# Last layer of a four-layer network: softmax bias, norms and expert weights on GpSimd, the experts' last product on VectorE

## The chip, the cores and the metric

The kernel runs on one core of a Trainium2 chip. The metric is the time of one execution on the device in microseconds (us); the time given is the median of several executions. Engines are named as the profile names them: PE is TensorE (PEld its weight loads), DVE is VectorE, ACT is ScalarE, POOL is GpSimd, SP issues the transfers. PSUM is the memory that PE writes; in this kernel's last layer it is used as eight banks of 128 x 512 numbers. The granted clock of PE is printed in every profile as a share of full speed.

## What is computed

The network has four layers; each adds a cross-attention block and then a feed-forward block to x, which is 2048 rows (16 tiles of 128) by 256. Only the last layer is touched:

```python
# cross-attention: 16 heads of 16, every row attends to all 2048 rows of ctx
q, k, v = _fq_sym(q * scale, -1), _fq_sym(k, -1), _fq_sym(v, 2)   # quantised to +-127
attn = softmax(q @ k.T)
attn = _fq_unsigned(attn, -1)                                     # quantised to 0..255 by its row's maximum
x = x + (attn @ v) @ Wp + bp
# mixture of experts: 8 experts of width 176, and 2 shared ones
probs = softmax(h @ gate_w.T);  w, selected = top_k(probs, 2)     # h: layernorm of x
w = w / (w.sum(-1) + 1e-20)
y_e = (silu(h @ gate_e.T) * (h @ up_e.T)) @ down_e.T              # every expert on every row
x = x + sum over e of combine[e] * y_e                            # shared experts have weight 1
```

## The kernel before

The last layer is the function `l3`, which begins about 1825 us into the execution and runs to its end. Its order is written out by hand for all engines (`manual_schedule`), so every engine works through its instructions in the order of the Python code.

The main loop `for u in range(N + 29)` runs over N = 256 pairs of a tile t and a head: u = 16 t + head. One pass is called a **round** here, and round h of a tile means u mod 16 = h. A softmax row has 2048 scores, which fill four banks; each quarter is a **piece** q = 0..3. In round u the engines get, in this order:

- ACT: four exponentials of head u (`exponentials`, L976), one for each piece, with the bias `nb` of that head. The result is rounded to 16-bit integers, and a transposing DMA from SP turns it (L980).
- PE: pieces 2 and 3 of head u+1 (`scores`, L954). DVE: their row maxima, negated (`peak`, L960), and then `bias` of head u+1: the smallest of the four columns of `nm` (L965), times the row's scale plus a constant (L966). The exponentials of round u+1 need it.
- the steps of the table `steps` that are due for some tile in this round (below).
- PE: the product of head u-4 with the values (`values`, L988), then pieces 0 and 1 of head u+2. DVE: the maximum of piece 0 of head u+2, then the second half of an expert if there is one (`rest`), then the maximum of piece 1.

Seven banks go round among the pieces and all other products. `take` chooses the free bank whose estimated return (`give`) is earliest. While an expert runs, its bank, given back in `rest` as u + 1.1, is the one that piece 2 of the next round takes.

The steps of tile t, at rounds counted from 16 t: -16 `stats`, -15 `norm` (L1003), -14 `turn_h`, -13 `project_q`, -12 `quant_q` (with four wide POOL operations and a memset, L1034 to L1039), -6 `turn_q`; 20 `divide` (L1055 to L1060), 21 `turn_o`, 22 `project_o`, 23 `stats_m`, 24 `norm_m` (L1089), 25 `turn_m`, 27 `logits`, 28 `top`, 29 `combine` (L1118 to L1125); 30 to 39 the ten experts; 33, 36, 39, 40 `turn_a`, the transposes of the experts' results `act`; 40, 41, 43, 44 `down`, the last projection.

So round h of the loop holds, for three tiles at different stages: h = 14, 15, 0 to 7 one expert each; beside it in h = 0 `stats`, 1 `turn_a` and `norm`, 2 `turn_h`, 3 `project_q`, 4 `turn_a`, `divide` and `quant_q`, 5 `turn_o`, 6 `project_o`, 7 `turn_a` and `stats_m`; h = 8 `turn_a`, `down`, `norm_m`; 9 `down`, `turn_m`; 10 `turn_q`; 11 `down`, `logits`; 12 `down`, `top`; 13 `combine`.

An expert is: PE multiplies into one bank `gu` (gate in the left half, up in the right, L243); ACT writes tanh of the left half to `ma` (L1133) and the right half times the expert's weight to `mb` (L1134); DVE makes (ma + 1) * left half (L1137); POOL multiplies that by `mb` into `act` (L1138). The order of a round's work with an expert in it, as in the code:

```python
for f in steps.get(...): later.append(f(t, u))     # PE: gu; ACT: ma, mb
values(u - LAG)                                    # PE
for q in range(2): scores(u + 2, q)                # PE: pieces 0 and 1
peak(u + 2, 0)                                     # DVE
for f in later: f()                                # DVE: L1137, POOL: L1138 (rest)
peak(u + 2, 1)                                     # DVE
```

The feed-forward block of the first layer (L441 to L443) already computes its experts with ACT for the tanh alone and two DVE products, both of 128 x 176.

Of the kernel before, what the change touches and what calls it, by code (L numbers as in the profile page):

```python
# [18 lines left out]
F32 = mybir.dt.float32  # L19
BF16 = mybir.dt.bfloat16  # L20
# [4 lines left out]
AF = mybir.ActivationFunctionType  # L25
ALU = mybir.AluOpType
AX = mybir.AxisListType
PSUM = bass.MemoryType.PSUM

P = 128  # L30
NT = 16
D = 256
NH = 16
T = NT * P

MAGIC = 12582912.0
LN255 = 5.541263545158426
# [3 lines left out]
class Net:  # L41
# [879 lines left out]
    def l3(self, w3, moe_w):  # L921
# [7 lines left out]
        nc, tc = self.nc, self.tc  # L929
        qw, ow, qb, ob, kst, v, sv = (w3[n] for n in ("q", "o", "qb", "ob", "k", "v", "sv"))  # L930
        gate_w, wgu, wd = moe_w
        NE, IN = 10, 176
        LAG = 4
        E = mybir.EngineType
        with (self.pool("l3x", bufs=2) as pool, self.pool("l3p", bufs=3) as pp,
              self.pool("l3t", bufs=LAG + 1) as tp, self.pool("l3m", bufs=1) as mp,
              self.pool("l3e", bufs=3) as ep):
            st = {}
# [3 lines left out]
            def take(shape, name, dtype=F32):  # L942
                tag = min(banks, key=banks.get)
                del banks[tag]
                return self.bank(shape, tag, name, dtype), tag

            def give(tag, when):
                banks[tag] = when


            def scores(u, q):
                t, hd = divmod(u, NH)
                ps, tag = st["s", u, q] = take([P, 512], "piece")
                nc.tensor.matmul(ps, qTs[t % 2][:, hd, :],  # L954
                                 kst[q // 2][:, hd // 2, 512 * (q % 2):512 * (q % 2) + 512], start=True, stop=True)

            def peak(u, q):
                if q == 0:
                    st["nm", u] = self.s(4, "nm")
                nc.vector.tensor_reduce(st["nm", u][:, q:q + 1], st["s", u, q][0], AX.X, ALU.max, negate=True)  # L960

            def bias(u):
                t, hd = divmod(u, NH)
                nb = st["nb", u] = self.s(1, "nb")
                nc.vector.tensor_reduce(nb, st.pop(("nm", u)), AX.X, ALU.min)  # L965
                nc.vector.tensor_scalar(nb, nb, st["sq", t][:, hd:hd + 1], LN255, ALU.mult, ALU.add)  # L966

            def exponentials(u):
                t, hd = divmod(u, NH)
# [30 lines left out]

            def norm(t, u):
                st["h"] = pool.tile([P, D], F32, name="ln_h", tag="ln_h")
                nc.vector.tensor_scalar(st["h"], self.x[t], st["mv"][:, 0:1], st["r"], ALU.subtract, ALU.mult)  # L1003

            def turn(src, n, name, where, u):

# [18 lines left out]
            def quant_q(t, u):  # L1025
                q = st["q"]
                v = q.rearrange("p (h d) -> p h d", d=16)
                am, s4, r, sq = self.s(NH, "ham"), self.s(NH, "hs4"), self.s(NH, "hr"), self.s(NH, "hs")
                nc.vector.tensor_reduce(am, v, AX.X, ALU.max, apply_absolute_value=True)

                nc.vector.tensor_scalar(s4, am, 1.0 / 127.0, 4e-8, ALU.mult, ALU.max)
                nc.vector.reciprocal(r, s4)
                nc.gpsimd.tensor_scalar(sq, s4, 0.25, None, ALU.mult)
                nc.gpsimd.tensor_tensor(v, v, r.unsqueeze(2).to_broadcast([P, NH, 16]), ALU.mult)  # L1034
                nc.gpsimd.tensor_scalar(q, q, MAGIC, None, ALU.add)
                qi = pool.tile([P, NH, 64], BF16, name="qi", tag="qi")
                nc.gpsimd.memset(qi[:, :, 48:], 0.0)
                for j in range(3):
                    nc.gpsimd.tensor_scalar(qi[:, :, 16 * j:16 * j + 16], v, -MAGIC, None, ALU.add)  # L1039
                st["qi"], st["sq", t] = qi, sq  # L1040

            def turn_q(t, u):
                out = qTs[t % 2].rearrange("p (j two) q -> p j two q", two=2)
# [9 lines left out]
            def divide(t, u):  # L1053
                rz, z = self.s(NH, "rz"), st.pop(("z", t))
                nc.vector.tensor_reduce(rz, z, AX.X, ALU.add)  # L1055
                nc.vector.reciprocal(rz, rz)
                nc.vector.tensor_scalar(rz, rz, 2.0 ** 24, None, ALU.mult)
                st["out"] = pool.tile([P, NH, 16], F32, name="o", tag="o")
                nc.vector.tensor_tensor(st["out"], st.pop(("av", t)), rz.unsqueeze(2).to_broadcast([P, NH, 16]), ALU.mult)  # L1059
                nc.gpsimd.tensor_tensor(self.x[t], self.x[t], ob, ALU.add)  # L1060
# [25 lines left out]

            def norm_m(t, u):
                st["mh"] = mp.tile([P, D], F32, name="mh", tag="mh")
                nc.vector.tensor_scalar(st["mh"], self.x[t], st["mmv"][:, 0:1], st["mr"], ALU.subtract, ALU.mult)  # L1089

            def turn_m(t, u):
                st["mhT"] = turn(st["mh"], 2, "mhT", mp, u)
# [21 lines left out]
            def combine(t, u):  # L1114
                best, fidx = st["best"], st["fidx"]

                den, w = self.s(1, "gden"), self.s(2, "gw")
                nc.vector.tensor_scalar(den, best[:, 0:1], best[:, 1:2], 1e-20, ALU.add, ALU.add)  # L1118
                nc.vector.reciprocal(den, den)
                nc.vector.tensor_scalar(w, best[:, :2], den, 0.5, ALU.mult, ALU.mult)  # L1120
                comb, one = mp.tile([P, NE], F32, name="comb", tag="comb", bufs=2), self.s(8, "gone")
                nc.vector.tensor_scalar(comb[:, :8], self.iota[:, :8], fidx[:, 0:1], w[:, 0:1], ALU.is_equal, ALU.mult)
                nc.vector.tensor_scalar(one, self.iota[:, :8], fidx[:, 1:2], w[:, 1:2], ALU.is_equal, ALU.mult)
                nc.vector.tensor_tensor(comb[:, :8], comb[:, :8], one, ALU.add)
                nc.gpsimd.memset(comb[:, 8:], 0.5)  # L1125
                st["comb"] = comb

            def expert(e):
                def step(t, u):
                    ps, tag = take([P, 2 * IN], "gu")  # L1130
                    self.matmul_acc(ps, [(st["mhT"][:, c, :], wgu[:, c, e, :]) for c in range(2)])
                    a, b = (ep.tile([P, IN], F32, name=n, tag=n) for n in ("ma", "mb"))
                    nc.scalar.activation(a, ps[:, :IN], AF.Tanh, scale=0.5)  # L1133
                    nc.scalar.activation(b, ps[:, IN:], AF.Identity, scale=st["comb"][:, e:e + 1])  # L1134

                    def rest():
                        nc.vector.scalar_tensor_tensor(a, a, 1.0, ps[:, :IN], ALU.add, ALU.mult)  # L1137
                        nc.gpsimd.tensor_tensor(act[:, e * IN:(e + 1) * IN], a, b, ALU.mult)  # L1138
                        give(tag, u + 1.1)
                    return rest  # L1140
                return step
# [7 lines left out]
            def down(k):  # L1149
                def step(t, u):  # L1150
# [7 lines left out]
                    if k == 3:  # L1158
# [3 lines left out]
                return step  # L1162


            steps = {-16: [stats], -15: [norm], -14: [turn_h], -13: [project_q], -12: [quant_q], -6: [turn_q],
                     20: [divide], 21: [turn_o], 22: [project_o],
                     23: [stats_m], 24: [norm_m], 25: [turn_m], 27: [logits], 28: [top], 29: [combine]}
            for e in range(NE):
# [7 lines left out]
            act = mp.tile([P, 14 * P], F32, name="act", tag="act")  # L1176
# [2 lines left out]
            qTs = [mp.tile([P, NH, P], BF16, name=f"qT{j}", tag=f"qT{j}") for j in range(2)]  # L1179
            with tc.manual_schedule(engines={E.PE, E.DVE, E.Activation, E.Pool, E.SP}):  # L1180
                nc.gpsimd.memset(act[:, NE * IN:], 0.0)
                for qT in qTs:
                    nc.gpsimd.memset(qT, 0.0)
                for n in sorted(n for n in steps if n < 0):
                    for f in steps[n]:
                        f(0, -1)
                for q in range(4):
                    scores(0, q)
                    peak(0, q)
                bias(0)  # L1190
                for q in range(2):
                    scores(1, q)
                    peak(1, q)
                for u in range(N + 29):
                    if u < N:
                        exponentials(u)
                    if u + 1 < N:
                        for q in (2, 3):
                            scores(u + 1, q)
                            peak(u + 1, q)  # L1200
                        bias(u + 1)
                    later = []
                    for t in range(NT):
                        for f in steps.get(u - NH * t, ()) if u - NH * t >= 0 or t > 0 else ():
                            later.append(f(t, u))
                    if 0 <= u - LAG < N:
                        values(u - LAG)
                    for q in range(2):
                        if u + 2 < N:
                            scores(u + 2, q)  # L1210
                    if u + 2 < N:
                        peak(u + 2, 0)
                    for f in later:
                        if f:
                            f()
                    if u + 2 < N:
                        peak(u + 2, 1)
# [83 lines left out]
```

## Time and profile before

| | |
|---|---|
| median of three executions | 2978.15 us (2968.15 to 2980.59) |
| profiled execution, its own time | 2982.18 us |
| span in the profile | 2980.4 us |
| mean granted clock of PE over the span | 0.918 |
| stretch 1850 to 2930 us, 1080 us: busy PE / DVE / ACT / POOL | 837.4 / 873.0 / 929.1 / 177.9 us |
| the same stretch: mean granted clock | 0.89 |

The exponentials of round 0 start at 1849.5 us and those of the last round at 2929.9 us. From one round's first exponential to the next round's, the medians of tiles 4 to 14 are, in us:

| round h | 0 | 1 | 2 | 3 | 4 | 5 | 6 | 7 |
|---|---|---|---|---|---|---|---|---|
| us | 3.74 | 4.20 | 4.01 | 3.76 | 4.76 | 6.19 | 3.75 | 4.77 |

| round h | 8 | 9 | 10 | 11 | 12 | 13 | 14 | 15 |
|---|---|---|---|---|---|---|---|---|
| us | 3.29 | 4.84 | 3.99 | 6.27 | 3.30 | 4.18 | 4.99 | 3.74 |

Four exponentials by themselves take 3.02 to 3.04 us a round (the rounds 0 to 13 of the first tile, where there is little else, are mostly of that length). Sixteen rounds take 68.6 to 71.4 us in tiles 2 to 14. Rounds 5, 11 and 15 differ from tile to tile (5.23 to 6.82, 4.62 to 6.88, 3.73 to 5.27 us); the others hardly do.

In a row of the timeline the columns are: start in us, duration in us, engine, line, operation, out<-in, shape, how many were merged into the row, and in brackets how long the engine stood idle before it and what ended that.

### The profile page before, as it was taken

The numbers are of one execution on the slowest core, as the hardware profiler recorded it, in microseconds if no ns is written. First come the engines' busy times: TensorE is split into PE (matmuls) and PEld (weight loads), VectorE is DVE, ScalarE is ACT, GpSimd is POOL, SyncE is SP. The second block draws the span as 40 slices with busy tenths as digits, with TensorE's granted clock in tenths as the row PEclk, the third lists the DMA queues.
The fourth block names the chain that finished last, engine by engine and source line by source line (L and its number), as shares of the span: only waits on it lengthen the run. The fifth ranks groups of instructions, "written<-read, shape, count | busy, mean of one in ns | idle before, by whom it ended". The sixth has DMA issues, their size and how long they took to land. (4 is left out here: it accounts for less than half of the span.)

```text
span 2980.4 us, 41726 instructions
## 1 busy us (share of the span) xinstructions
PE 2462.4 (83%) x14070; PEld 1558.7 (52%) x14070; DVE 1969.7 (66%) x5045; ACT 1758.9 (59%) x4636; POOL 1000.2 (34%) x1587
## 2 busy tenths in 40 slices
PE   5888998999999877888888885777777777777778
PEld 4555666666666544456555652344444444444445
DVE  4555665655665634566666644987887788777774
ACT  1344444444444432555555542988888888888884
POOL 4443444444443322555555531111111111121111
PEclk8889999999999898899999996689999899899999
DMA  6000000000001011000000003876766666666672
GB/s 207 1 1 1 1 1 1 1 1 1 1 1 36 23 35 41 5 5 5 5 5 5 1 1 94 154 130 122 129 125 122 122 123 128 121 125 117 122 128 57
DMA packets 559830, 171.38 MB, mean 58 GB/s; under 512 B 538912, under 2 KB 555904, under 8 KB 558848
## 3 DMA queue, kind: packets, MB, share of 16 engines
q1 hardware_dynamic: 559616, 168.72, 28.0%
q8 instruction: 111, 1.82, 0.2%
q14 instruction: 103, 0.84, 0.1%
HBM read 32.37 MB, written 2.10 MB: 12 GB/s over the span
## 5 line engine op out<-in xcount | busy, mean ns | idle before, releaser
L976 ACT ACTIVATE p<-piece,nb,hs 128x512 int16<-128x512 f32 x1024 | 785.3, 791 | 27.6 <-issue 16.9
L960 DVE TENSOR_REDUCE nm<-piece 128x1 f32<-128x512 f32 x1024 | 651.9, 684 | 110.0 <-PE piece L954 101.6
L954 PE MATMUL piece<-kst,qT 128*128 128x512 bf16 x1024 | 367.9, 415 | 200.9 <-DVE ma L1137 89.3
L1138 POOL TENSOR_TENSOR act<-ma,mb 128x176 f32<-128x176 f32 x160 | 89.1, 558 | 764.1 <-DVE ma L1137 763.1
L243 PE MATMUL gu<-w_L_ffn_wgu,mhT 128*128 128x352 f32 x640 | 254.1, 526 | 11.5 <-ACT p L976 8.0
L954 PEld LDWEIGHTS <-qT 128*128 128x128 bf16 x1024 | 77.1, 98 | 298.9 <-issue 169.8
L235 ACT COPY pT<-tp 128x512 f32<-128x512 f32 (+1 forms) x208 | 116.1, 563 | 185.1 <-PE tp L219 184.2
L976 ACT ACTIVATION_READ_ACCUMULATOR p<-piece,nb,hs 128x1 f32 x1024 | 222.7, 217 | 0.0
L243 PEld LDWEIGHTS gu<-w_L_ffn_wgu,mhT 128*128 128x128 f32 x640 | 124.3, 208 | 132.2 <-ACT p L976 83.9
L988 PEld LDWEIGHTS <-pT 128*128 128x128 f16 x4096 | 143.9, 99 | 81.8 <-issue 66.7
L270 POOL TENSOR_TENSOR kx<-kT,hmask 128x512 f32<-128x512 f32 x128 | 133.1, 1048 | 152.1 <-PE scores L273 102.3
L534 ACT ACTIVATE s<-s,nb,qs 128x128 f32<-128x128 f32 x256 | 123.2, 482 | 97.5 <-DVE nb L532 95.8
L289 PEld LDWEIGHTS av<-v,pT 128*128 128x128 f32 x1024 | 133.6, 198 | 87.5 <-ACT pT L235 73.3
L243 PE MATMUL gu<-w_L_ffn_wgu,hT 128*128 128x352 f32 x512 | 174.5, 463 | 0.9 <-ACT actT L235 0.6
L289 PE MATMUL av<-v,pT 128*128 128x17 f32 x1024 | 134.8, 263 | 47.8 <-ACT pT L235 47.7
L275 DVE TENSOR_REDUCE mx<-scores 128x4 f32<-128x512 f32 x128 | 88.2, 689 | 120.1 <-PE scores L273 119.6
L280 ACT ACTIVATE p<-scores,mx,qs 128x128 f32<-128x128 f32 x256 | 96.9, 459 | 118.8 <-DVE mx L278 111.2
L988 PE MATMUL av<-v_int,pT 128*128 128x16 bf16 x4096 | 143.4, 171 | 19.3 <-DVE o L1059 19.3
L273 PE MATMUL scores<-kx,qT 128*128 128x512 f32 x256 | 153.8, 686 | 3.1 <-ACT qT L235 2.7
L537 POOL TENSOR_TENSOR s<-s,rz 128x512 f32<-128x512 f32 x64 | 66.7, 1043 | 227.5 <-DVE rz L536 225.2
L549 PE MATMUL oproj<-w_L_ffn_oT,oT 128*128 128x256 f32 x512 | 130.4, 399 | 4.9 <-ACT oT L543 4.8
L243 PE MATMUL q<-w_L_ffn_qT,hT 128*128 128x512 f32 x256 | 126.7, 598 | 2.2 <-DVE rot L488 2.1
(362 smaller groups left out, 5375.4 us busy)
## 6 DMA issues: line engine op xcount, KB each, us to landing
pT<-p SPq DMA_TRANSPOSE x256, 4.3
w_L_ffn_wgu<-in_L_ffn_wgu SPq DMA_DIRECT2D x1, 3520.0 KB, 12.0
w_L_ffn_wgu<-in_L_ffn_wgu SPq DMA_DIRECT2D x1, 2816.0 KB, 9.4
x<-in_x SPq DMA_DIRECT2D x16, 128.0 KB, 4.6
ctxT<-in_ctxT SPq DMA_DIRECT2D x4, 512.0 KB, 5.3
w_L_ffn_qT<-in_L_ffn_qT SPq DMA_DIRECT2D x1, 2048.0 KB, 12.2
w_L_ffn_oT<-in_L_ffn_oT SPq DMA_DIRECT2D x1, 2048.0 KB, 17.1
ctx<-in_ctx SPq DMA_DIRECT2D x16, 128.0 KB, 2.0
```

The source lines that it names most:

```text
L235: nc.scalar.copy(out[:, j0:j0 + m, :], ps)
L243: self.nc.tensor.matmul(ps, a, b, start=(j == 0), stop=(j == n - 1))
L270: nc.gpsimd.tensor_tensor(kx, kT[oc].unsqueeze(1).to_broadcast([P, 4, P]), self.hmask[:, hs].unsqueeze(2).to_broadcast([P, 4, P]), ALU.mult)
L273: nc.tensor.matmul(ps, qT[:, oc, :], kx, start=True, stop=True)
L280: nc.scalar.activation(p[:, h, :], ps[:, h, :], AF.Exp, bias=mx[:, h:h + 1], scale=scale)
L289: nc.tensor.matmul(av[:, 4 * g + h, :], pT[:, h, :], v[:, 4 * g + h, :], start=True, stop=True)
L534: nc.scalar.activation(s[:, j, :], s[:, j, :], AF.Exp, bias=nb[:, j:j + 1], scale=qs[:, j:j + 1], accum_out=z[:, j:j + 1])
L549: nc.tensor.matmul(proj, oT[:, j, :], w["o"][:, c, :], start=(c == 0), stop=(c == 15))
L954: nc.tensor.matmul(ps, qTs[t % 2][:, hd, :], kst[q // 2][:, hd // 2, 512 * (q % 2):512 * (q % 2) + 512], start=True, stop=True)
L960: nc.vector.tensor_reduce(st["nm", u][:, q:q + 1], st["s", u, q][0], AX.X, ALU.max, negate=True)
L976: nc.scalar.activation(p[:, 512 * q:512 * q + 512], ps, AF.Exp, bias=nb, scale=st["sq", t][:, hd:hd + 1], accum_out=st["z", t][:, hd, q:q ...
L988: nc.tensor.matmul(st["av", t][:, hd, :], pb[:, c, :], v[:, c, hd * 16:(hd + 1) * 16], start=(c == 0), stop=(c == NT - 1))
```

## The change

- The running minimum of the four `nm` columns and the bias move to POOL: after the maximum of piece 1 and of piece 2 POOL takes a minimum of two columns into a fifth and sixth column; `bias` becomes two POOL operations (minimum with the last column and product with the scale; plus the constant) in place of two DVE operations.
- `norm` and `norm_m` (layernorm of 128 x 256) move from DVE to POOL.
- In `combine` the four operations after the reciprocal move from DVE to POOL.
- An expert loses ACT's `mb` and POOL's product. DVE makes the second product itself, up half of the bank times the expert's weight times `ma`, straight into `act`.
- `quant_q` is cut in pieces: its last five POOL operations move to the four rounds that follow (`round_q`, `copy_q`).
- The factor 2^24 that `divide` multiplied in once a tile (L1057) goes once into `sv`, before the loop.

```diff
             def peak(u, q):
                 if q == 0:
-                    st["nm", u] = self.s(4, "nm")
-                nc.vector.tensor_reduce(st["nm", u][:, q:q + 1], st["s", u, q][0], AX.X, ALU.max, negate=True)
+                    st["nm", u] = self.s(6, "nm")
+                nm = st["nm", u]
+                nc.vector.tensor_reduce(nm[:, q:q + 1], st["s", u, q][0], AX.X, ALU.max, negate=True)
+                if q in (1, 2):
+
+                    nc.gpsimd.tensor_scalar(nm[:, 3 + q:4 + q], nm[:, q:q + 1], nm[:, 0:1] if q == 1 else nm[:, 4:5],
+                                            None, ALU.min)
 
             def bias(u):
                 t, hd = divmod(u, NH)
                 nb = st["nb", u] = self.s(1, "nb")
-                nc.vector.tensor_reduce(nb, st.pop(("nm", u)), AX.X, ALU.min)
-                nc.vector.tensor_scalar(nb, nb, st["sq", t][:, hd:hd + 1], LN255, ALU.mult, ALU.add)
+                nm = st.pop(("nm", u))
+                nc.gpsimd.tensor_scalar(nb, nm[:, 3:4], nm[:, 5:6], st["sq", t][:, hd:hd + 1], ALU.min, ALU.mult)
+                nc.gpsimd.tensor_scalar(nb, nb, LN255, None, ALU.add)
...
             def norm(t, u):
                 st["h"] = pool.tile([P, D], F32, name="ln_h", tag="ln_h")
-                nc.vector.tensor_scalar(st["h"], self.x[t], st["mv"][:, 0:1], st["r"], ALU.subtract, ALU.mult)
+                nc.gpsimd.tensor_scalar(st["h"], self.x[t], st["mv"][:, 0:1], st["r"], ALU.subtract, ALU.mult)
...
                 nc.gpsimd.tensor_scalar(sq, s4, 0.25, None, ALU.mult)
                 nc.gpsimd.tensor_tensor(v, v, r.unsqueeze(2).to_broadcast([P, NH, 16]), ALU.mult)
+                st["sq", t] = sq
+
+            def round_q(t, u):
+                q = st["q"]
                 nc.gpsimd.tensor_scalar(q, q, MAGIC, None, ALU.add)
-                qi = pool.tile([P, NH, 64], BF16, name="qi", tag="qi")
+                qi = st["qi"] = pool.tile([P, NH, 64], BF16, name="qi", tag="qi")
                 nc.gpsimd.memset(qi[:, :, 48:], 0.0)
-                for j in range(3):
-                    nc.gpsimd.tensor_scalar(qi[:, :, 16 * j:16 * j + 16], v, -MAGIC, None, ALU.add)
-                st["qi"], st["sq", t] = qi, sq
+
+            def copy_q(j):
+                def step(t, u):
+                    v = st["q"].rearrange("p (h d) -> p h d", d=16)
+                    nc.gpsimd.tensor_scalar(st["qi"][:, :, 16 * j:16 * j + 16], v, -MAGIC, None, ALU.add)
+                return step
...
                 nc.vector.reciprocal(rz, rz)
-                nc.vector.tensor_scalar(rz, rz, 2.0 ** 24, None, ALU.mult)
...
-                nc.vector.tensor_scalar(st["mh"], self.x[t], st["mmv"][:, 0:1], st["mr"], ALU.subtract, ALU.mult)
+                nc.gpsimd.tensor_scalar(st["mh"], self.x[t], st["mmv"][:, 0:1], st["mr"], ALU.subtract, ALU.mult)
...
-                nc.vector.tensor_scalar(w, best[:, :2], den, 0.5, ALU.mult, ALU.mult)
+                nc.gpsimd.tensor_scalar(w, best[:, :2], den, 0.5, ALU.mult, ALU.mult)
...
-                nc.vector.tensor_scalar(comb[:, :8], self.iota[:, :8], fidx[:, 0:1], w[:, 0:1], ALU.is_equal, ALU.mult)
-                nc.vector.tensor_scalar(one, self.iota[:, :8], fidx[:, 1:2], w[:, 1:2], ALU.is_equal, ALU.mult)
-                nc.vector.tensor_tensor(comb[:, :8], comb[:, :8], one, ALU.add)
+                nc.gpsimd.tensor_scalar(comb[:, :8], self.iota[:, :8], fidx[:, 0:1], w[:, 0:1], ALU.is_equal, ALU.mult)
+                nc.gpsimd.tensor_scalar(one, self.iota[:, :8], fidx[:, 1:2], w[:, 1:2], ALU.is_equal, ALU.mult)
+                nc.gpsimd.tensor_tensor(comb[:, :8], comb[:, :8], one, ALU.add)
...
-                    a, b = (ep.tile([P, IN], F32, name=n, tag=n) for n in ("ma", "mb"))
+                    a, w = ep.tile([P, IN], F32, name="ma", tag="ma"), st["comb"][:, e:e + 1]
                     nc.scalar.activation(a, ps[:, :IN], AF.Tanh, scale=0.5)
-                    nc.scalar.activation(b, ps[:, IN:], AF.Identity, scale=st["comb"][:, e:e + 1])
 
                     def rest():
                         nc.vector.scalar_tensor_tensor(a, a, 1.0, ps[:, :IN], ALU.add, ALU.mult)
-                        nc.gpsimd.tensor_tensor(act[:, e * IN:(e + 1) * IN], a, b, ALU.mult)
+                        nc.vector.scalar_tensor_tensor(act[:, e * IN:(e + 1) * IN], ps[:, IN:], w, a, ALU.mult, ALU.mult)
                         give(tag, u + 1.1)
...
-            steps = {-16: [stats], -15: [norm], -14: [turn_h], -13: [project_q], -12: [quant_q], -6: [turn_q],
+            steps = {-16: [stats], -15: [norm], -14: [turn_h], -13: [project_q], -12: [quant_q], -11: [round_q],
+                     -10: [copy_q(0)], -9: [copy_q(1)], -8: [copy_q(2)], -6: [turn_q],
...
                 nc.gpsimd.memset(act[:, NE * IN:], 0.0)
+                nc.vector.tensor_scalar(sv, sv, 2.0 ** 24, None, ALU.mult)
```

The order of instructions on PE, and so the bank that each product takes, is the same in both kernels.

## The prediction

> **What bounds the kernel.** The last layer, 1849 to 2930 us, is nearly all that the change touches. Busy shares (ACT 929, DVE 873, PE 837 of 1080 us) name no bound; the medians of the rounds do: with one expert and little else a round takes 3.74 us, though four exponentials need 3.03. I read the timeline of all engines for such a round (15), then the list of waits.
>
> ```profile
> 2306.48 0.59 PE L954 MATMUL piece<-kst,qT 128*128 128x512 bf16 x2
> ...
> 2306.90 0.69 DVE L960 TENSOR_REDUCE nm<-piece 128x1 f32<-128x512 f32 x1 [0.43 <-PE piece L954]
> 2307.50 0.33 DVE L1137 SCALAR_TENSOR_TENSOR ma<-ma,gu 128x176 f32<-128x176 f32 x1
> ...
> 2307.89 0.61 PE L954 MATMUL piece<-kst,qT 128*128 128x512 bf16 x2 [0.81 <-DVE ma L1137]
> ...
> 2308.53 1.45 PE L243 MATMUL gu<-w_L_ffn_wgu,mhT 128*128 128x352 f32 x4
> ...
> 2310.07 0.32 ACT L1133 ACTIVATE ma<-gu 128x176 f32<-128x176 f32 x1
> ...
> 2310.22 0.59 PE L954 MATMUL piece<-kst,qT 128*128 128x512 bf16 x2
> 2310.29 0.40 ACT L1134 ACTIVATE mb<-gu,comb 128x176 f32<-128x176 f32 x1
> ...
> 2310.58 0.78 ACT L976 ACTIVATE p<-piece,nb,hs 128x512 int16<-128x512 f32 x1
> ```
> ```profile
> PE piece L954 <- DVE ma L1137: 88.0, 137, 0.9
> PE piece L954 <- ACT p L976: 73.7, 158, 1.5
> ```
>
> Two loops close at 3.74 us. **The bank loop**: piece 0 (2306.48), its maximum (+0.42), the expert's DVE product (+0.60), which frees the bank that piece 2 of the next round takes (+0.39), those two pieces (to the next expert's gu, +0.64), gu and the values, then piece 0 again (+1.69). **The ACT loop**: second exponential, its bank to gu, gu, `ma`, `mb`, exponential. PE stands idle 0.81 us each time for L1137, and gu follows the pieces within 0.03 (2308.50, 2308.53): the bank loop has at most 0.03 us to spare. What the reader is to see: DVE and ACT both have idle time in this round, and yet the round is as long as the chain through the one bank.
>
> **The second product, the main term.** The bank is now free only after two DVE products. The trace holds the same pair, on the same shape, in the first layer's feed-forward:
>
> ```profile
> 417.25 0.34 DVE L442 SCALAR_TENSOR_TENSOR ma<-ma,gu 128x176 f32<-128x176 f32 x1 [0.46 <-ACT ma L441]
> 417.63 0.40 DVE L443 SCALAR_TENSOR_TENSOR act<-ma,comb,gu 128x176 f32<-128x176 f32 x1
> ```
>
> The second starts 0.38 after the first and takes 0.40: the release comes 0.78 after L1137's start and not 0.33, **0.45 later**. Bounds: 0.25 (the spacing of DVE operations that don't depend on each other, L1137 to the next maximum) to 0.55 (0.10 for the two waits of the new product, on the first product and on POOL's `comb`). I take the pair's own spacing, since it is the same two operations. Behind the piece that waits stand, on PE, piece 3, the next gu, the values and the next piece 0, so the whole round moves with it; behind the new product DVE has only the maximum of piece 1, which is not late. Round by round, from piece 0 to piece 0, 0.45 less the slack of gu after the pieces (it waited for ACT there, which gets earlier):
> - to rounds 15, 0, 1: slack 0.03, so 3 x 0.42.
> - to 2 and 3: slack 0.11 (pieces done 2316.38, gu 2316.49), so 2 x 0.34.
> - to 4: the values wait for `o` of `divide` (PE idle 1.18). DVE's chain gains 0.45, loses the two bias operations (0.32, 2257.47 to 2257.79) and L1057 (0.21): -0.08. PE's own work before the values ends at 2257.92, 0.45 later still before `o`.
> - to 5 and 7: no slack, 2 x 0.45. To 6: slack 0.32, 0.13.
> - to 8: the transposes no longer wait for POOL's product, and the bank of `down` waits for an exponential anyway: 0.
>
> Sum 2.89 us a tile. ACT's loss of `mb` (0.29 from its start to the next, 2310.29 to 2310.58) lies beside this: the ACT loop shrinks to 3.45 and ACT waits the rest of the new 4.16. POOL's product (0.56) goes too; POOL is busy 178 of 1080 us, and nothing in the loop but round 8's transposes waited for it.
>
> **The bias on POOL.** Before, from the end of the last maximum to the exponential: 0.04 + 0.20 + 0.21 + 0.09 = 0.54. On POOL: 0.09 to start (ln_mv to L187), two dependent operations of 0.26 and 0.20 with 0.08 between (L187 takes 0.19; a 128x1 product, L747, 0.24), 0.09 to ACT: 0.72, bounds 0.60 and 1.2 (POOL's cost of a several-fold wait isn't shown). In expert rounds ACT waits for gu far longer. The exponentials wait for the bias at the ends of rounds 9 and 12, +0.18 each, and of 13, where DVE's chain loses 0.33 of the earlier bias: -0.15. Sum +0.21. The running minima wait for DVE's maxima, with the bias queued behind them; 0.09 + 0.26 after each maximum, they are done before the last one ends, 0.63 after its predecessor.
>
> **The rest costs nothing.** The layernorms take 0.94 on POOL (below) for 0.40 on DVE; their transposes come 3.4 us later or more. Without that cover, 0.5 each. `combine` takes some 1.2 us on POOL for 1.3 on DVE, and the first second product comes 4 us later. `quant_q`'s tail, 0.86 + 0.31 + 3 x 0.85, ends in round 8 instead of 5, `turn_q` in round 10; in one piece it would have held up the bias behind it by 3.7 us. POOL has per round four small operations (0.9) and at most 1.8 of these: under 4.16, and each batch starts just after a bias. No DMA is moved.
>
> ```profile
> L735 POOL TENSOR_SCALAR k<-k,n 128x256 f32<-128x256 f32 x16 | 15.1, 941 | 0.2
> ```
>
> Here the Trainium skill speaks against the change: GPSIMD Engine Reference, section 4.1, sends elementwise work to VectorE, GpSimd being about 2 times slower with two inputs and at line rate with one. With one tensor input this row is 2.3 times L1003 (404 ns). By the rule the norm costs 0, by the row 0.54; hidden both ways.
>
> **Ends.** The prologue's norm is bare: +0.5. After the last exponential three waits of PE for `act` (2964.94, 2969.58, 2970.76) lose `mb` and POOL's 0.56 and gain one DVE product, about -0.6 each; `combine` there is +0.4. Together -0.9.
>
> **Sum.** 14 tiles have their experts inside the loop (tile 14 has two in it, where no pieces follow, and tile 15 none): 14 x (2.89 + 0.21) = 43.4; less 0.9, +42.5. The profiled execution's own 2982.2 becomes 3024.7; it lies 4.0 above the median shown, so the median becomes **3021 us**.
>
> **The clock.** PE's idle gap grows from 0.81 to 1.26. Windows of 3.413 us, cut at the multiples at which the granted clock switches:
>
> ```profile
> 2306.44:2309.85 3.41, 2.56 (x18) 1.06 (x15) 2.91 (x7) 3.41 (x10) 0.56 (x1) 1.00 0.76 146
> 2350.81:2354.22 3.41, 1.98 (x27) 1.13 (x27) 2.50 (x6) 3.41 (x10) 0.00 (x0) 1.00 0.47 90
> 2354.22:2357.64 3.42, 2.61 (x7) 1.69 (x7) 3.29 (x6) 3.08 (x9) 0.00 (x0) 0.50 0.82 158
> 2214.28:2217.69 3.41, 2.00 (x29) 1.29 (x28) 2.41 (x6) 3.41 (x8) 0.00 (x0) 1.00 0.55 87
> 2217.69:2221.11 3.42, 3.16 (x31) 2.39 (x30) 2.51 (x7) 2.20 (x9) 0.00 (x0) 1.00 0.65 135
> ```
>
> After window and length come PE's busy us; near the end PEclk. 1.98 busy is followed by half clock, 2.00 is not; in this layer the edge lies near 0.60 of a window. TensorE: Matmul & The Clock Gate (HAM oscillation) warns of idle gaps over some 3.4 us: by it a gap of 1.26 costs nothing. By the trace an expert window falls from 2.56 to (3.41 - 1.29) = 2.12, 0.62: just above the edge, so I take 0, but 0.08 us more gap would cross it.
>
> **Rivals.**
> - *Clock cascade.* For: that margin. Against: by the matmuls' rows, four of five windows between 0.61 and 0.63 in this layer were followed by full clock. A round at half clock takes 5.26 (2232.48 to 2237.74), so 5.7 with the product, 1.5 above 4.16. With four more such rounds a tile, 14 x 4 x 1.5 = 84: 3105.
> - *ACT sets the pace, faster.* For: ACT is the busiest, and the chain of waits is mostly exponentials. If the bank of the expert weren't the one PE waits for, 0.29 would go in each of 140 expert rounds: 2978 - 41 = 2937. It decides if the added DVE time in the loop is under 0.03 us. Against: 137 waits for L1137, 88 us.
> - *Bias late.* If the POOL chain takes 1.2, rounds 9, 12 and 13 lose 0.5 more: 14 x 1.5 = 21, so 3042. For: four dependent operations in one queue. Against: POOL is nearly idle.
> - *The change doesn't do what it says*: no sign of it; PE's order is unchanged, and ACT, DVE and POOL hold the operations that the diff names.
>
> **Chances.** Forecast 0.56, cascade 0.19, bias late 0.09, ACT pace 0.11, the terms cancelling within 0.5% (15 us, what a measurement of this kernel can tell from none) 0.05. Slower 0.84, same 0.05, faster 0.11. The forecast's own range is 2996 (0.25 for the product: 1.16 a tile in place of 2.89) to 3040 (0.55: 3.89 a tile, 3035, and the clock a little worse). That holds the bias case nearly too. Reaching half into the cascade above, and a little into the cancelling case below, the range is 2992 to 3090; outside lie the ACT pace and the long half of the cascade.
>
> **What would show it.** PE's idle before the pieces of an expert round, behind the new product, should be about 1.26, the expert round 4.16, ACT idle 0.7 before `ma` there, round 13 a little shorter, PEclk near 0.89. Wrong if expert rounds shrink to 3.45; if pieces wait less than 1.0; if half-clock windows crowd the rounds 14 to 2; if exponentials wait for POOL in expert rounds.

## The result, and the profile after

The changed kernel takes **3008.6 us** (median of 6 runs, 3003.48 to 3014.78), the kernel before 2975.8 us beside it (6 runs, 2968.15 to 2981.78): ratio 1.0121, 95% interval 1.0100 to 1.0142. It is 33 us slower; the forecast was 43. The profiled execution has a span of 3013.1 us for 2980.4, so the two traces differ by 32.7 us. Of that, 35.2 us is there when the last head's piece 0 starts (2958.1 us for 2922.9); the tail gives 2.5 back.

The timeline of all engines for the same plain expert round that the forecast read (round 15, at full clock; start, duration, engine, line, operation, and in brackets the idle time before it and what ended it):

```profile
2466.94 0.59 PE L954 MATMUL piece<-kst,qT 128*128 128x512 bf16 x2
...
2467.35 0.69 DVE L961 TENSOR_REDUCE nm<-piece 128x1 f32<-128x512 f32 x1 [2.10 <-PE piece L954]
...
2467.96 0.33 DVE L1148 SCALAR_TENSOR_TENSOR ma<-ma,gu 128x176 f32<-128x176 f32 x1
2468.32 0.40 DVE L1149 SCALAR_TENSOR_TENSOR act<-gu,comb,ma 128x176 f32<-128x176 f32 x1
...
2468.64 1.88 DVE L961 TENSOR_REDUCE nm<-piece 128x1 f32<-128x512 f32 x3
...
2468.78 0.60 PE L954 MATMUL piece<-kst,qT 128*128 128x512 bf16 x2 [1.25 <-DVE act L1149]
...
2469.22 1.35 PE L243 MATMUL gu<-w_L_ffn_wgu,mhT 128*128 128x352 f32 x4
...
2470.40 0.55 PE L994 MATMUL av<-v_int,pT 128*128 128x16 bf16 x16
...
2470.60 0.32 ACT L1145 ACTIVATE ma<-gu 128x176 f32<-128x176 f32 x1 [0.52 <-PE gu L243]
2470.72 0.36 POOL L971 TENSOR_SCALAR nb<-nm,hs 128x1 f32<-128x1 f32 x1 [0.36 <-DVE nm L961]
...
2470.81 0.59 PE L954 MATMUL piece<-kst,qT 128*128 128x512 bf16 x2
...
2471.17 0.22 POOL L972 TENSOR_SCALAR nb<-nb 128x1 f32<-128x1 f32 x1
...
2471.42 0.78 ACT L982 ACTIVATE p<-piece,nb,hs 128x512 int16<-128x512 f32 x1 [0.50 <-POOL nb L972]
```

The reader is to see two things. The pieces wait 1.25 us for the second product where they waited 0.81 for the first, and from piece 0 (2466.94) to piece 0 (2470.81) the round takes 3.87 us for 3.74. And a wait is new: the last maximum ends at 2470.52, the bias at 2471.39, and ACT's exponential stands 0.50 us for it.

The list of waits in the stretch from 2000 to 2900 us, first PE's, then ACT's (us in total, times, longest):

```profile
PE piece L954 <- DVE act L1149: 146.1, 121, 1.4
PE piece L954 <- ACT p L982: 64.0, 128, 1.4
```
```profile
ACT ma L1145 <- PE gu L243: 92.3, 104, 2.6
ACT p L982 <- POOL nb L972: 53.0, 92, 0.9
```

In the same stretch of the kernel before, the same two waits were shorter, and no exponential waited for a bias:

```profile
PE piece L954 <- DVE ma L1137: 82.8, 129, 0.9
```
```profile
ACT ma L1133 <- PE gu L243: 60.0, 57, 2.6
```

The windows view of the last layer shows PE, DVE and ACT less busy than before, POOL more, and the same mean clock, 0.89:

```profile
1850.00:2960.00 1110.00, 812.47 (x6553) 471.84 (x6553) 814.30 (x1638) 895.90 (x2331) 449.49 (x1293) 0.89 0.66 122
```

**How rounds are compared below.** From each trace I took the time from piece 0 of one round to piece 0 of the next, and how much of it lay in windows at half clock. Medians over those instances of a round (tiles 2 to 14) that have no half clock in them agree between kernels to 0.02 us where nothing was changed (rounds 10 and 11: 5.08 us, and 3.39 to 3.41, in every kernel with spare matmuls below). So they show what an edit does by itself; the half-clock time, given in us a tile (mean of tiles 3 to 13), stands beside them. "From 14 to 15" means from piece 0 of round 14 to piece 0 of round 15.

### The profile page after: what moved, and what is told of

Read it like the earlier page. It is cut to its first block, busy times and chain, and to the rows that moved or that the text cites. A ratio compares the mean times of both kernels' runs of the same rounds, so it can differ in the third digit from the quotient of the medians.

```text
span 3013.1 us, 42599 instructions
## 1 busy us (share of the span) xinstructions
PE 2440.6 (81%) x14070; PEld 1561.2 (52%) x14070; DVE 1919.9 (64%) x4582; ACT 1723.5 (57%) x4476; POOL 1266.9 (42%) x2547
## 3 DMA queue, kind: packets, MB, share of 16 engines
q8 instruction: 111, 1.82, 0.2%
## 4 chain that ended last, share of the span: by engine, by line
PE 54%; DVE 22%; ACT 11%; POOL 7%; issue 4%; DMA 1%; DVEq 0%; SPq 0%; ACTq 0%; POOLq 0%
PE gu L243 10%; DVE nm L961 8%; PE tp L219 6%; ACT p L982 5%; PE piece L954 4%; PE oproj L549 4%; PE q L243 4%; PE scores L273 4%; PE av L289 3%; PE moe L1168 3%; PE moe L243 2%; PE out L243 2%; PE oT L541 2%; DVE act L1149 2%; PE av L994 2%
## 5 line engine op out<-in xcount | busy, mean ns | idle before, releaser
L964 POOL TENSOR_SCALAR nm<-nm 128x1 f32<-128x1 f32 x512 | 145.0, 283 | 533.3 <-DVE nm L961 530.0
L982 ACT ACTIVATION_READ_ACCUMULATOR p<-piece,nb,hs 128x1 f32 x1024 | 208.2, 203 | 0.0
L243 PEld LDWEIGHTS gu<-w_L_ffn_wgu,mhT 128*128 128x128 f32 x640 | 133.5, 215 | 102.7 <-ACT p L982 44.3
L971 POOL TENSOR_SCALAR nb<-nm,hs 128x1 f32<-128x1 f32 x256 | 93.2, 364 | 93.6 <-DVE nm L961 58.4
## 6 DMA issues: line engine op xcount, KB each, us to landing
w_L_ffn_qT<-in_L_ffn_qT SPq DMA_DIRECT2D x1, 2048.0 KB, 11.5
```

Source lines behind the costliest of these rows:

```text
L243: self.nc.tensor.matmul(ps, a, b, start=(j == 0), stop=(j == n - 1))
L964: nc.gpsimd.tensor_scalar(nm[:, 3 + q:4 + q], nm[:, q:q + 1], nm[:, 0:1] if q == 1 else nm[:, 4:5], None, ALU.min)
L982: nc.scalar.activation(p[:, 512 * q:512 * q + 512], ps, AF.Exp, bias=nb, scale=st["sq", t][:, hd:hd + 1], accum_out=st["z", t][:, hd, q:q ...
```

## The experiments

All times are medians; before was run beside each group (2975.96 for e1 to e4, 2976.28 for the first four kernels with spare matmuls, 2972.64 for nomb and the two with the bias on VectorE, 2973.32 for w_early). Before itself differs by up to 3.6 us between these groups, so a difference of kernels from two groups is good to some 4 us.

| kernel | time us | ratio to before, 95% interval | half clock, us a tile | full-clock rounds, us a tile |
|---|---|---|---|---|
| before | 2975.8 | | 11.5 | |
| the change | 3008.6 | 1.0100 to 1.0142 | 10.6 | |
| e1_product | 2991.3 | 1.0041 to 1.0078 | 7.8 | |
| e2_no_product | 2966.2 | 0.9954 to 0.9982 | 7.5 | |
| e3_bias | 3039.0 | 1.0199 to 1.0237 | 16.1 | |
| e4_early | 3005.7 | 1.0077 to 1.0111 | 15.5 | |
| w_before | 2947.8 | 0.9892 to 0.9919 | 2.2 | 66.35 (65.88) |
| w_after | 2959.4 | 0.9937 to 0.9962 | 0.0 | 68.18 |
| w_e1 | 2968.7 | 0.9962 to 0.9987 | 2.2 | 67.98 (67.64) |
| w_e2 | 2928.6 | 0.9825 to 0.9854 | 0.0 | 65.75 |
| nomb | 2935.4 | 0.9842 to 0.9904 | 7.1 | |
| w_after_dvebias | 2954.6 | 0.9935 to 0.9966 | 1.6 | 67.51 |
| w_rest_dvebias | 2924.7 | 0.9815 to 0.9865 | 1.2 | 65.58 |
| w_early | 2973.0 | 0.9994 to 1.0021 | 5.1 | 66.20 |

The last column is left empty where some round of a tile never ran, or hardly ever, at full clock. In w_before and w_e1 the spare matmuls themselves lengthen the round from 14 to 15 (4.21 us for 3.74 and 3.87 at full clock without them); in brackets stands the sum with that taken out.

### The parts of the change, one at a time

**e1_product**: the kernel before, with the expert of the changed kernel.

```diff
-                    nc.scalar.activation(b, ps[:, IN:], AF.Identity, scale=st["comb"][:, e:e + 1])
...
-                        nc.gpsimd.tensor_tensor(act[:, e * IN:(e + 1) * IN], a, b, ALU.mult)
+                        nc.vector.scalar_tensor_tensor(act[:, e * IN:(e + 1) * IN], ps[:, IN:], w, a, ALU.mult, ALU.mult)
```

> The kernel before with the second product alone moved to VectorE (mb and POOL's product gone, bias, norms and combination as before). Bank theory (the later release of the expert's bank is the cost): the 2.89 us a tile of the forecast, and 0.5 more to round 4, because the divide keeps the bias operations ahead of it: 14 x 3.4 less 1.8 at the end, +46, about 3022. PE's wait for the new product about 1.25 us each time. If the bias on POOL were the larger cost of the change, this kernel would lie under 2990.

Measured 2991.3: 15 above before, a third of what I expected. The pieces wait as long as foreseen (148.8 us in 127 waits), but the rounds grow less, and half clock fell from 11.5 to 7.8 us a tile.

**e2_no_product**: the changed kernel with the expert as before (the diff above, the other way round).

> The changed kernel with the expert's product as before (mb on ACT, last product on POOL), all else of the change kept. Bank theory: within 6 us of before (2970 to 2982), since only 0.21 us a tile is left for the bias and the divide gets earlier by about 0.5. If the bias on POOL is what costs, it stays near 3000. Exponentials waiting for POOL's bias: at the ends of rounds 9 and 12 only.

Measured 2966.2: 10 faster than before, just under the range. ACT did wait for the bias in more places than I named (29.5 us in 58 waits). Here too half clock fell, to 7.5 us a tile. The two parts add up to +5, the whole change is +33: something that doesn't add is at work.

**e3_bias**: the kernel before with `peak` and `bias` of the changed kernel, nothing else.

> The kernel before with minimum and bias alone on POOL. Bank theory: +0.18 at two rounds of a tile, -0.3 at the divide: 2970 to 2980. Bias theory: four dependent POOL operations make every exponential that follows ma late, 0.4 us in some ten rounds of a tile, +50, about 3025.

Measured 3039.0, worse than either theory allowed, and for neither's reason. The timeline of POOL at round 4 to 5, with the exponential that follows:

```profile
2500.28 0.87 POOL L1041 TENSOR_SCALAR q<-q 128x256 f32<-128x256 f32 x1
2501.09 0.31 POOL L1043 MEMSET qi<- 128x256 bf16 x1
2501.37 2.49 POOL L1045 TENSOR_SCALAR qi<-q 128x256 bf16<-128x256 f32 x3
2503.83 0.56 POOL L1144 TENSOR_TENSOR act<-ma,mb 128x176 f32<-128x176 f32 x1
2504.37 0.68 POOL L964 TENSOR_SCALAR nm<-nm 128x1 f32<-128x1 f32 x2
2505.16 0.37 POOL L971 TENSOR_SCALAR nb<-nm,hs 128x1 f32<-128x1 f32 x1
2505.61 0.23 POOL L972 TENSOR_SCALAR nb<-nb 128x1 f32<-128x1 f32 x1
...
2505.87 0.78 ACT L982 ACTIVATE p<-piece,nb,hs 128x512 int16<-128x512 f32 x1 [1.20 <-POOL nb L972]
```

The tail of `quant_q` holds POOL's queue for 3.55 us (2500.28 to 2503.83), and the minima and the bias stand behind it. PE runs short meanwhile, half clock rises to 16.1 us a tile, and the round from 5 to 6 takes 8.07 us (mean) for 4.78. With the tail cut into four rounds (e2) the same bias leaves the kernel 10 faster than before. e2 differs from e3 in the norms, `combine` and the scale of `divide` too, so the cut by itself was not tried; but the timeline shows nothing else of that length ahead of the bias.

### The bank freed early

**e4_early**: the changed kernel, with the product taken in another order.

```diff
-                    a, w = ep.tile([P, IN], F32, name="ma", tag="ma"), st["comb"][:, e:e + 1]
+                    a, b = (ep.tile([P, IN], F32, name=n, tag=n) for n in ("ma", "mb"))
                     nc.scalar.activation(a, ps[:, :IN], AF.Tanh, scale=0.5)
+                    nc.vector.tensor_scalar(b, ps[:, IN:], st["comb"][:, e:e + 1], None, ALU.mult)
+                    nc.vector.tensor_tensor(b, ps[:, :IN], b, ALU.mult)
+                    give(tag, u + 1.1)
...
-                        nc.vector.scalar_tensor_tensor(a, a, 1.0, ps[:, :IN], ALU.add, ALU.mult)
-                        nc.vector.scalar_tensor_tensor(act[:, e * IN:(e + 1) * IN], ps[:, IN:], w, a, ALU.mult, ALU.mult)
-                        give(tag, u + 1.1)
+                        nc.vector.scalar_tensor_tensor(act[:, e * IN:(e + 1) * IN], a, 1.0, b, ALU.add, ALU.mult)
```

> The changed kernel with the expert's product taken in another order: VectorE multiplies the up half by the weight and then by the gate half as soon as gu is there, which frees the bank without waiting for the maximum of piece 0; (tanh + 1) times that comes where the second product was. VectorE does three operations for an expert where the change does two, about 0.33 us more. Bank theory: PE no longer waits for the product, an expert round falls to 3.5 to 3.75 us (ACT's 4 exponentials and ma, 3.4, with the handshakes; or VectorE's 2.5 + 1.1), so 10 x 14 x 0.4 to 0.7 below the changed kernel: 2915 to 2955, below the kernel before too. If VectorE's load as such is the cost, 10 x 14 x 0.33 = 46 above it: about 3055.

Measured 3005.7, level with the change (their ranges overlap): a miss. The waits of PE (2000 to 2900 us) show that the bank did come free early; those of ACT show what took its place:

```profile
PE piece L954 <- DVE mb L1147: 17.0, 55, 0.4
```
```profile
ACT p L982 <- POOL nb L972: 69.2, 104, 1.1
```

Expert rounds now alternate (3.36 us from 14 to 15, in the one instance at full clock, and 4.51 from 15 to 0), and half clock is 15.5 us a tile. Which of the two ate the gain is taken up again below, with w_early.

### The clock taken out

The windows of 3.413 us around round 10 of the kernel before (PE busy, PEld, DVE, ACT, POOL; then the granted clock):

```profile
2490.74:2494.15 3.41, 1.82 (x28) 1.13 (x27) 2.40 (x6) 3.41 (x8) 0.00 (x0) 1.00 0.35 70
2494.16:2497.57 3.41, 3.34 (x10) 2.29 (x7) 2.50 (x6) 1.94 (x6) 0.00 (x0) 0.50 0.81 119
```

PE is busy 1.82 of 3.41 us while ACT runs without a pause; the next window has half clock, and the projection in it pays for it (round 10 takes 6.61 us in the mean, 5.09 at full clock). The next four kernels fill such holes with matmuls that nothing needs:

```diff
+            WARM = {(10, 2): 1, (10, 3): 1, (10, 0): 5, (13, 0): 2, (13, 1): 2, (14, 2): 6, (14, 3): 1}
+            def keep(u, q):
...
+                spare = st["av", t][:, hd + 1:, :].rearrange("p h d -> p (h d)")
+                for _ in range(n):
+                    nc.tensor.matmul(spare, self.ident, wd[:, 0, :m], start=True, stop=True)
...
                             scores(u + 1, q)
+                            keep(u, q)
...
                             scores(u + 2, q)
+                            keep(u, q)
```

> The kernel before with spare matmuls on PE where it waits for ACT in rounds 10, 13 and 14 (18 a tile, fp32, constant operands, into columns of the accumulator of values that a later head writes anew); nothing else is touched and no engine but PE has more to do. Clock theory: windows of 3.413 us in which PE is under some 0.6 busy are followed by half clock, and rounds 10, 13 and 14 pay about 1.5 + 1.3 + 0.5 us a tile for it; with the spare matmuls half-clock time in these rounds falls from 9.0 us a tile to under 3, and the time by 25 to 50: 2925 to 2950. Rival (half clock there costs nothing, because ACT is waited for anyway): 2976 or more.

Measured 2947.8, 28 faster than before. The same round 10, by windows and on PE's timeline:

```profile
2475.99:2479.41 3.42, 3.21 (x31) 2.53 (x28) 2.57 (x5) 3.42 (x9) 0.00 (x0) 1.00 0.71 97
2479.41:2482.82 3.41, 2.99 (x29) 2.00 (x28) 2.50 (x7) 2.19 (x7) 0.00 (x0) 1.00 0.77 156
```
```profile
2476.40 1.39 PE L992 MATMUL av<-w_L_ffn_wd,ident 128*128 128x144 f32 x10
```

The spare matmuls stand in the hole, no half clock follows, and round 10 takes 5.08 us, as it did at full clock without them. The clock theory holds.

> The changed kernel with the same spare matmuls. Clock theory: with the clock out of it the change costs the sum of its full-clock rounds, 2.48 us a tile, 14 x 2.48 = 35 more than the kernel before with spare matmuls (30 to 42). Rival (the clock has no part in the comparison): the same, 33; the pair e1 and e2 tells them apart.

> The second product alone, with the same spare matmuls. Clock theory: its full-clock rounds are 1.71 us a tile longer than before's, so 24 above before with spare matmuls (18 to 30), where without them it was 15. Rival (the product really costs 15, and the other 28 of the change come from the two parts together): 15 again, 12 to 17.

> The change without the product, with the same spare matmuls. Clock theory: its full-clock rounds sum to 0.1 us a tile less than before's, so its lead of 10 over before came from the clock and shrinks to 0 to 4. Rival: 10 faster than before with spare matmuls, as without them.

Measured 2959.4, 2968.7 and 2928.6: 12 above w_before, 21 above it, and 19 below it. Only the product came as expected. The differences of the medians mislead here, because w_before and w_e1 keep 2.2 us a tile of half clock in round 4, where no spare matmul stands, and pay 0.47 and 0.34 us in round 14 for the spare ones, while w_after and w_e2 have neither. The full-clock rounds don't have these flaws: 65.88 before, 67.64 with the product alone (+1.76), 65.75 without it (-0.13), 68.18 for the whole change (**+2.30**). The +1.76 and the -0.13 are the 1.71 and -0.1 that were read before these runs; but at 1.63 together the parts still fall short of 2.30.

### The bias, with and without the product

**w_after_dvebias** and **w_rest_dvebias**: the changed kernel, and the changed kernel without the product, both with spare matmuls, both with `peak` and `bias` as before:

```diff
-                nc.gpsimd.tensor_scalar(nb, nm[:, 3:4], nm[:, 5:6], st["sq", t][:, hd:hd + 1], ALU.min, ALU.mult)
-                nc.gpsimd.tensor_scalar(nb, nb, LN255, None, ALU.add)
+                nc.vector.tensor_reduce(nb, st.pop(("nm", u)), AX.X, ALU.min)
+                nc.vector.tensor_scalar(nb, nb, st["sq", t][:, hd:hd + 1], LN255, ALU.mult, ALU.add)
```

> The changed kernel with spare matmuls, but minimum and bias on VectorE as in the kernel before; product, norms, combination and the split tail of quant_q stay as changed. Theory that the bias on POOL is late by about 0.37 us where an exponential waits for it: rounds 8 and 12 get 0.4 shorter each, 14 and 15 about 0.1, round 3 (divide behind the bias operations) 0.3 longer: 6 below the changed kernel with spare matmuls, 2950 to 2957. Theory that the bias on POOL pays for itself: 2960 or more.

> As the changed kernel without the product and with spare matmuls, but minimum and bias on VectorE too: what is left of the change is norms, combination and quant_q's tail on POOL in pieces, and the scale moved out of divide. If these give what the part without the product gained (19 below before with spare matmuls), about 2930; if it was the bias leaving VectorE ahead of the divide, only round 3's 0.2 is left, about 2944.

Measured 2954.6 and 2924.7. In full-clock rounds the account now closes:

- norms, combination, the cut tail of `quant_q` and the scale out of `divide`: 65.88 to 65.58, **-0.30** us a tile;
- the product on top of that: 65.58 to 67.51, **+1.93**;
- the bias on POOL on top of both: 67.51 to 68.18, **+0.67**; without the product it costs 65.75 - 65.58 = 0.17.

Together +2.30. The bias costs more beside the product. That fits ACT being ready sooner without `mb`: the exponentials waited for it 92 times, with `mb` (e2) 58 times. w_rest_dvebias is the fastest version tried, 1.6% under the kernel before, with w_e2 close to it; half of that or more is the clock (w_before alone gave 0.9%). Of its 23 us under w_before only some 4 are the norms and the rest (0.30 x 14); 0.47 us a tile is w_before's round 14, and 1.0 us a tile less is spent at half clock.

### The bank loop by itself

**nomb**: the kernel before without `mb`.

```diff
-                    nc.scalar.activation(b, ps[:, IN:], AF.Identity, scale=st["comb"][:, e:e + 1])
...
-                        nc.gpsimd.tensor_tensor(act[:, e * IN:(e + 1) * IN], a, b, ALU.mult)
+                        nc.gpsimd.tensor_tensor(act[:, e * IN:(e + 1) * IN], a, a, ALU.mult)
```

> The kernel before without mb: ACT doesn't read the up half, and POOL multiplies ma by itself, so the up half of every expert is left out of the result. What is left at a plain expert round is the bank loop by itself. Theory that gu had 0.20 us of slack behind the pieces (it waited there for ACT's second exponential, 0.64 after piece 2, where 0.44 is enough): 3.74 falls to about 3.54 at full clock, and rounds 14 to 0 with it. The forecast's reading (at most 0.03 of slack): 3.71.

Measured 2935.4, and the rounds from 14 to 0 take 3.44 + 3.61 = 7.05 us at full clock, 3.53 each, for 3.74. PE's timeline of such a round:

```profile
2494.75 0.60 PE L954 MATMUL piece<-kst,qT 128*128 128x512 bf16 x2 [0.81 <-DVE ma L1136]
2495.19 1.35 PE L243 MATMUL gu<-w_L_ffn_wgu,mhT 128*128 128x352 f32 x4
```

`gu` starts 0.44 us after piece 2, before the recorded end of the pieces (2495.35), where it stood at 0.64 in the kernel before. The bank loop had 0.20 us of slack that my reading hid.

The traces of both kernels show the same without nomb, in the row of the weight load of `gu` (PEld), which the forecast's reading left out. First the kernel before in the round that the forecast read, then the changed kernel in the round shown after the result:

```profile
2308.53 0.89 PEld L243 LDWEIGHTS gu<-w_L_ffn_wgu,mhT 128*128 128x128 f32 x4 [0.53 <-ACT p L976]
```
```profile
2469.01 1.00 PEld L243 LDWEIGHTS gu<-w_L_ffn_wgu,mhT 128*128 128x128 f32 x4
```

Before, the weights of `gu` waited for an exponential; after, they follow the pieces without a wait, and `gu` starts 0.44 us after piece 2 (2468.78 to 2469.22). At full clock in tiles 2 to 14 of the kernel before, the medians of that distance are 0.64 us in rounds 0 and 1, 0.69 and 0.70 in rounds 2 and 3 and 0.94 in round 6, always with this wait, and 0.43 to 0.44 without it in rounds 4, 5 and 7. In the changed kernel they are 0.43 to 0.44 in all of these rounds.

### The early bank with the clock taken out

**w_early**: e4_early with the spare matmuls.

> The changed kernel with the product in the other order (bank free early, as in e4) and with the spare matmuls. e4 took the wait for the product away (17 us of PE's waits in place of 146) and was no faster; its full-clock rounds sum to 65.7 us a tile, 2.4 below the changed kernel's 68.2, but it spent 15.5 us a tile at half clock. Theory that half clock ate the gain: with the spare matmuls it is some 30 below the changed kernel with them, 2920 to 2940 (round 4's half clock stays). Theory that the bias on POOL took the product's place as the bound (exponentials waited 69 us for it): 2950 or more.

Measured 2973.0, 14 above w_after (17 by the ratios to before): a miss. The number lies where the second theory put it, but the rounds do not bear that theory out: at full clock, waits for the bias included, they are 2.0 us a tile shorter than w_after's (66.20 for 68.18). But w_early has 5.1 us of half clock a tile left, in rounds where no spare matmul stands (4, 5, 7 and 1; round 7 takes 5.3 us, and 7.2 where a half-clock window falls into it), and w_after has none. Its mean tile is 68.77 us for 68.26. Exponentials wait 75.0 us for the bias (2000 to 2900 us). So half clock took the gain of the full-clock rounds here too; what the waits for the bias cost besides wasn't tried.

## Why the forecast came out as it did

Terms of the forecast beside the full-clock rounds, w_after less w_before, with the flaw of w_before's round 14 taken out (us a tile; the table's round is the one the time leads to):

| to round | 15, 0, 1 | 2, 3 | 4 | 5, 7 | 6 | 8, 9, 10 | 13 | 14 | sum |
|---|---|---|---|---|---|---|---|---|---|
| forecast | 3 x 0.42 | 2 x 0.34 | -0.08 | 2 x 0.45 | 0.13 | 0.18 | 0.18 | -0.15 | 3.10 |
| measured | 0.27, 0.25, 0.21 | 2 x 0.13 | -0.14 | 0.51, 0.44 | -0.08 | 0.37 | 0.38 | -0.16 | 2.31 |

- **The mechanism was right, and shown.** The pieces wait for the second product; the bank comes 0.82 us after the first product's start (2467.96 to 2468.78) where it came after 0.39, 0.43 later for the 0.45 forecast. PE's gap of 1.26 was measured as 1.25.
- **The step that failed** is the slack, "the bank loop has at most 0.03 us to spare". It was read from the recorded end of the pieces; but `gu` waited there for ACT's second exponential, and without `mb` ACT frees that bank earlier. By nomb and by the weight loads the slack is 0.20 us more. The six terms that lean on it (to 15, 0, 1, 2, 3 and 6) make 2.07 us in the forecast and 0.87 with 0.20 taken from each. The product alone (w_rest_dvebias to w_after_dvebias) measures 0.72 for them: 0.20, 0.19 and 0.37 to rounds 15, 0 and 1, 0.06 each to 2 and 3, -0.16 to 6. To rounds 4, 5 and 7, which had no such slack, it measures 0.43, 0.43 and 0.44 for the 0.45 forecast. An expert round at full clock takes 3.87 to 4.0 us, not 4.16.
- **The bias** was put at 0.72 us from the last maximum to the exponential; in the round shown it takes 0.90 (2470.52 to 2471.42: 0.20 to start, 0.36 and 0.22 for the two operations and 0.09 between, 0.03 to ACT). It was also placed wrongly: at the end of round 9, where 0.18 was forecast, it costs nothing (3.36 us to round 10 in w_after and in w_after_dvebias); it costs 0.47 at the end of round 8, which the forecast didn't name, and 0.38 for the 0.18 forecast at the end of round 12. The sign that was to refute the forecast, exponentials that wait for POOL in expert rounds, is there: 52 of the 92 waits are in rounds 0 to 7. In the rounds from 14 to 2 the bias cost little all the same, 0.23 us together by the same two kernels.
- **Two errors partly cancel, and that is luck.** Split by what was moved, the forecast's 3.10 us are 3.42 for the product, -0.11 for the bias (0.21, less the 0.32 by which round 4 loses its two operations on DVE) and -0.21 for L1057. Measured are 1.93, 0.67 and, for all the rest, -0.30. The product was priced 1.5 too high, the bias 0.8 too low.
- **The clock** was taken as nothing. Between these two kernels it nearly is: 11.5 and 10.6 us of half clock a tile, mean 0.89 in both. But that is two changes that cancel, which nothing in the forecast foresaw: round 10 lost 2.7 us of it (4.2 to 1.6), the rounds from 13 to 15 gained 2.8 (4.8 to 7.6). For e1 and e2 it doesn't cancel, and that is why the parts of the change, measured without the spare matmuls, didn't add up. The cascade rival named the right place, rounds 14 and on, but not the size.
- **The rest at nothing** holds: norms, combination and the tail in pieces, with L1057 gone from `divide`, leave 0.30 us a tile on the good side, 0.20 of it to round 4. The norm took 1.25 us for the 0.94 it was priced at, and stayed hidden. That the uncut tail would hold the bias up by 3.7 us was measured in e3: 3.55.
- **The end** gave 2.5 us for the 1.4 forecast for it (three times 0.6, less 0.4).

The size follows: 14 tiles x 2.30 = 32.2, less 2.5 at the end, is 29.7 of the 32.7 us between the traces. The remaining 3 us, in the first tiles and in where half clock falls, I didn't separate. Why the half-clock windows fall where they do in each kernel stays open: moving the windows against the loop wasn't tried.

## What to carry to other kernels

Read the slack of a closed loop from an instance in which nothing else ends the wait, or by an experiment that relieves the other loop; when two loops close at the same length, the gap that looks like work in one may be a wait of the other. Here the row of the weight load showed that wait, and the rows of the matmuls alone did not. An operation moved to an idle engine is charged at the whole route from its producer to its consumer, and the long operations already in that queue must be cut before it goes there. Where PE idles for ACT, compare rounds at full clock before adding up parts, and try a few spare matmuls in the holes: here they took 28 us off the kernel before, where the change had added 33.

## What the runs showed of the hardware

- **Half clock after a sparse window.** Over the 14 traces, in the last layer: of the windows at full clock with PE busy for less than 0.50 of the window's 3.413 us, 197 of 201 were followed by half clock; between 0.50 and 0.56, 82 of 100; between 0.56 and 0.58, 31 of 49; between 0.58 and 0.60, 10 of 121; above that, 16 of 3291. Back to full clock it went after 319 of 332 windows with PE busy 0.90 or more, after 12 of 23 between 0.88 and 0.90, and after 14 of 325 under 0.86. The Trainium skill (TensorE: Matmul & The Clock Gate, HAM oscillation) speaks of idle gaps of more than 3.4 us. Between 2000 and 2900 us no gap of PE was longer than 2.1 us in any of the traces (1.5 in the kernel before), so by that rule half clock would have cost nothing there; the windows show that it came, and the measurement decides.
- **What it costs.** 18 spare matmuls a tile took the half-clock time in the kernel before from 11.5 to 2.2 us a tile and 28 us from its time; in the changed kernel from 10.6 to 0 and 49 us (3008.6 to 2959.4).
- **A norm on POOL** took 1.25 us, where a product of the same shape (L735) takes 0.94 and DVE 0.40 (a group of the changed kernel, 2000 to 2900 us: busy us, mean ns, idle before):

```profile
L1009 POOL TENSOR_SCALAR ln_h<-x,ln_mv,ln_r 128x256 f32<-128x256 f32 x12 | 15.0, 1248 | 1.2
```

- **Two readers of one bank in turn.** In e4_early VectorE's first read of the expert's bank waited for ACT's tanh of the same bank, whose result it doesn't use, so reading "as soon as `gu` is there" meant after `ma`. Why the wait is there no run shows (2000 to 2900 us):

```profile
DVE mb L1146 <- ACT ma L1145: 87.5, 91, 2.8
```
